# Twenty hold points a pair instead of twelve for GpSimd's gathers in a graph-network kernel

## The chip, the cores and the metric

One core of a Trainium2 chip. The metric is the device time of one execution in microseconds (us); a kernel's time is the median of its runs. Engines are named as in the profile: PE is TensorE (PEld its weight loads, which overlap its matmuls), DVE VectorE, ACT ScalarE, POOL GpSimd, SP SyncE.

## The reference

A layer of a graph network with 12,500 nodes and 400,000 edges, the edges sorted by their target node. For each edge the layer-normed features of both ends and the edge's own 32 numbers go through a small two-layer network; each node takes the maximum over its edges and adds it to its input.

```python
        e_feat = jnp.concatenate([x[rol], x[col], edge_attr], axis=-1)
        h = jax.nn.relu(e_feat @ W1 + b1)
        v = h @ W2 + b2
        x_cand = jax.ops.segment_max(v, col, num_segments=num_nodes)
        return jnp.maximum(x_cand, x[:, -v.shape[-1]:])
    edge_index = jnp.stack([src, dst])
    h = jnp.maximum(_layernorm(x, axis=-1), 0.0)
    x = x + _L0_gnn_ref(h, edge_index, edge_attr_32, L0_gnn_W1, L0_gnn_b1, L0_gnn_W2, L0_gnn_b2)
```

The first five lines are the body of `_L0_gnn_ref`, whose `x` is the normed `h`; `rol` and `col` are the two ends of an edge.

## The kernel before, in words

The sorted edges are cut into four stripes, and each stripe into 196 chunks of 512 edges; one step works on a chunk of all four stripes, that is on 16 columns of 128 edges. The loop takes two chunks at a time, a pair, so there are 98 pairs. Most time is spent on one job: getting `h[src]`, the rows of the edges' source nodes, which lie anywhere in memory.

That job is split between two ways. Twelve of a chunk's 16 columns are gathered by GpSimd with one indirect DMA for each column of 128 rows (`gather`, line 179). The other four are computed on TensorE (`tile`, line 344): one-hot rows `hot`, made by VectorE and ScalarE from keys, are multiplied with the whole table `hs`, in 14 matmuls a tile (seven groups of rows, each in two parts that add up to full precision); VectorE then masks and reduces the result (lines 351 and 352). In 34 of the chunks, always the second one of a pair, a fifth column is computed this way, so that GpSimd gathers 11. The prediction calls a pair with that extra tile a nine-tile pair, the others eight-tile pairs. An eight-tile pair has 24 gathers, a nine-tile pair 23.

Rows of both ways are turned by VectorE into `ht` (lines 368 and 371) and multiplied with the first weights.

TensorE's order in one pair is fixed by hand (`manual_schedule`); each engine runs its instructions in the order in which the code issues them. For a pair it is:

- three groups of first-layer matmuls, line 773: of the edges' own features (point `ea`), of the target windows, and of the rows (`ht`). Each is 8 matmuls in the program and 16 records in the profile, 48 records in all
- 8 transposes of the pair before, line 669 (`tr`)
- three tiles, the last three of the pair's first chunk, line 344 (`a1`, `a2`, `a3`)
- the second layer, line 807, 16 records, and 8 matmuls of the pair before, line 686 (`lv`)
- the four tiles of the second chunk (`b0` to `b3`), the extra tile of a nine-tile pair, and the first tile of the next pair (`n0`)

The names in brackets are points: `passes` notes the last matmul of a group under the pair's number and a name. GpSimd does nothing in the loop but issue gathers, two chunks ahead or more. It is kept to TensorE's pace by holds: `hold` looks up a gather's number in its pair (0 to 23, first chunk and then second) in the table `HELD`, which names a point and how many pairs back it lies; after the loop each held gather gets a semaphore wait for that point. The pair's first gathers are held by points three pairs back, the others by points two pairs back. So gathers run well ahead of their use: the latest of them are used about one pair later.

Each gather also waits for the gather eight before it (one of eight DMA semaphores, `DMASW0` to `DMASW7`) and, where it starts a new buffer of three columns (there are 14), for the VectorE instruction that read the buffer last.

Of the kernel before, what the change touches and what calls it, by code (L numbers as in the profile page):

```python
# [46 lines left out]
A1 = 7  # L47
# [16 lines left out]
LATE = NCH - 8  # L64
PIECE = 2 * A0
GP = 3
HELD = {0: (3, 'b1'), 2: (3, 'b2'), 4: (3, 'b3'), 6: (3, 'n0'), 8: (2, 'ea'), 10: (2, 'ht'), 12: (2, 'tr'), 14: (2, 'a1'), 16: (2, 'a2'), 18: (2, 'a3'), 20: (2, 'lv'), 22: (2, 'b0')}
BANKS = 7
SOON = {(3, 0): 'a0', (3, 6): 'a2', (4, 0): 'a3', (4, 6): 'b0', (5, 0): 'b1', (5, 6): 'b2'}
ROUND = 12582912.0  # L70
# [13 lines left out]
def gnn_kernel(ctx, tc, x, src, src_mm, src_x, src_t, dst, dst_ext, lo, lo_c, ends_b, edge_attr, weights, w1, w2, b2, out):  # L84
# [129 lines left out]
    def passes(iteration, name, ins):  # L214

        passed[iteration, name] = ins

    def hold(c, i, ins):

        at = HELD.get(i + c % 2 * (K - MM))  # L220
        if at and c // 2 - at[0] >= 0:
# [9 lines left out]
    def bank(name):  # L231

        return ring[0].tile([P, C], F32, name=name, tag="bank", bufs=BANKS)
# [94 lines left out]
    def tile(c, m):  # L328

        if c not in MMC or m == MM and c not in MMX:  # L330
            return
        if m == 0:
            mm_rows[c] = early.tile([P, MM, D], F32, name="gm", bufs=4)
        if m < MM:
            hot = [hots[c][:, k, m * P:(m + 1) * P] for k in range(A1)]
            mask, row = masks[c][:, m], mm_rows[c][:, m]
        else:
            _, mask, spaces = extras.pop(c)
            hot = [spaces[k // 2][:, k % 2 * P:(k % 2 + 1) * P] for k in range(A1)]
            row = gh[c][-1][:, SOME - 1]  # L340
        po = bank("pv")[:, :D * A0]
        for k in range(A1):
            for part in range(2):
                ins = nc.tensor.matmul(po, hot[k], hs[:, part, k].rearrange("p f a -> p (f a)"),  # L344
                                 start=(k == 0 and part == 0), stop=(k == A1 - 1 and part == 1))
        if m == 0 and c % 2 == 0:
            passes(c // 2 - 2, "n0", ins)
        passes(c // 2 - 1, "ab"[c % 2] + str(m), ins)
        of_group = po.rearrange("p (f a) -> p f a", a=A0)
        one = early.tile([P, D, A0], F32, name="one", bufs=2)  # L350
        nc.vector.tensor_tensor(one, of_group, mask[:, None, :].to_broadcast([P, D, A0]), op=ALU.mult)  # L351
        nc.vector.tensor_reduce(row, one, axis=AX.X, op=ALU.max)  # L352
# [210 lines left out]
    with tc.tile_pool(name="edges", bufs=3) as pool, tc.tile_pool(name="edges_ps", bufs=1, space=PSUM) as ps:  # L563
# [260 lines left out]
        load_wide(wide[0][1], (pen_d, 0), 0, LOAD * C, nc.sync)  # L824
        one_hots_act(3)
        tile(2, 0)
        one_hots(3, 0, 2)
        tile(2, 1)
        one_hots(3, 2, BY_ACT.start)
        mask_of(3)  # L830
        raw_turn(3)
        tile(2, 2)
        make_block(0)
        tile(2, 3)
# [19 lines left out]
        for c in range(0, NCH - 4, 2):  # L854
# [14 lines left out]
            if c == LATE + 2:  # L869
                ea = pool.tile([P, LOAD * C], F32, name="ea", bufs=2)  # L870
# [123 lines left out]
        c = NCH - 4  # L994
# [192 lines left out]
```

## Time and profile before

| | us |
|---|---|
| median of 3 runs | 3587.91 |
| lowest and highest run | 3581.08, 3589.38 |
| the profiled execution, own time | 3575.96 |
| its span, first to last instruction | 3574.1 |
| PE, busy | 3241.7 |
| DVE, busy | 2223.2 |
| POOL, busy | 2207.4 |
| ACT, busy | 1578.5 |

The mean granted clock of TensorE over the span is 0.944 of full speed. Busy times of PE come from matmuls whose ends are modelled, so a busy PE isn't a PE at its peak. In the rows of the timeline the first number is the start in us from the span's beginning, the second the length in us, and the bracket says how long the engine was idle before the row's first instruction and what ended that; `x16` counts records. In a row of the windows view the stretch is followed by its length, each engine's busy time with its count of instructions, the granted clock, the DMA engines' share and GB/s.

### The profile page before, as it was taken

How to read it: one execution, taken by the hardware profiler on the slowest of the kernel's cores; microseconds unless marked ns; L12 is line 12 of the kernel's file. 1: busy time of each engine (PE TensorE's matmuls, PEld its weight loads, DVE VectorE, ACT ScalarE, POOL GpSimd, SP SyncE). 2: the span in 40 equal slices, each digit the busy share in tenths (PEclk: the TensorE clock that was granted, in tenths of full speed). 3: DMA queues.
4: the chain of work that ended last, by engine and by line, in shares of the span. 5: the costliest groups of instructions: out<-in, count | busy, mean ns of one | idle time of the engine just before them, and what ended most of it. 6: DMA issues, size and time to landing. Idle time of an engine off the chain costs nothing.

```text
span 3574.1 us, 55458 instructions
## 1 busy us (share of the span) xinstructions
PE 3241.7 (91%) x19141; PEld 2547.7 (71%) x19141; DVE 2223.2 (62%) x4215; ACT 1578.5 (44%) x2470; POOL 2207.4 (62%) x2337
## 2 busy tenths in 40 slices
PE   5899999989999998999999999989999999999987
PEld 3577777777777776777777767777777777777765
DVE  5456666666666666666666666656665666666655
ACT  3344444443534444444443434444444444444443
POOL 6666666665666666666666666666666666666662
PEclk8899999999999999999999999999999999999997
DMA  5322222222222222222222222222222222222222
GB/s 175 99 60 62 53 64 62 62 50 62 64 62 53 61 63 65 50 66 60 62 50 70 57 56 58 59 59 61 60 62 59 60 61 61 63 65 49 59 58 65
DMA packets 178819, 227.49 MB, mean 64 GB/s; under 512 B 109621, under 2 KB 150373, under 8 KB 165734
## 3 DMA queue, kind: packets, MB, share of 16 engines
q10 hardware_dynamic: 29828, 108.01, 9.6%
q0 software_dynamic: 74336, 38.21, 8.5%
q1 hardware_dynamic: 74370, 77.70, 7.0%
q8 instruction: 151, 2.47, 0.3%
q14 instruction: 134, 1.10, 0.1%
HBM read 212.23 MB, written 11.46 MB: 63 GB/s over the span
## 4 chain that ended last, share of the span: by engine, by line
PE 81%; issue 10%; DVE 6%; another core or an unknown queue 2%; SPq 1%; DMA 1%; ACT 1%; DVEq 0%; ACTq 0%
PE pv L344 60%; PE ph L773 10%; PE pv L686 4%; PE pv L669 3%; PE pv L807 3%; DVE hot L304 1%; DVE one L351 1%; DVE last L650 1%; DVE sm L815 1%; DMA top_d<-wo 0%; DVE ht L368 0%; SPq L616 0%; SPq L707 0%; SPq L625 0%
## 5 line engine op out<-in xcount | busy, mean ns | idle before, releaser
L179 POOL DMA_INDIRECT gh<-h_d,src_i x2291 | 2169.8, 947 | 1296.3 <-issue 560.0
L344 PE MATMUL pv<-hs,hot 128*128 128x448 f32 x10752 | 2373.0, 378 | 97.5 <-issue 83.9
L344 PEld LDWEIGHTS pv<-hs,hot 128*128 128x128 f32 x10752 | 2089.1, 196 | 345.7 <-issue 159.7
L351 DVE TENSOR_TENSOR one<-pv,mask 128x448 f32<-128x448 f32 x768 | 472.3, 615 | 1219.7 <-remote 464.7
L798 ACT ACTIVATE hid<-ph,wt 128x512 f32<-128x512 f32 x392 | 250.0, 688 | 1124.6 <-remote 498.2
L352 DVE TENSOR_REDUCE gm<-one 128x32 f32<-128x448 f32 x768 | 476.2, 620 | 26.5
L304 DVE TENSOR_TENSOR hot<-kb,consts 128x1024 fp32r<-128x1024 f16 (+1 forms) x379 | 447.5, 1199 | 0.0
L318 ACT ACTIVATE hot<-away,ones 128x512 fp32r<-128x512 f32 x582 | 421.6, 724 | 45.0 <-remote 26.1
L317 ACT ACTIVATE away<-kb,key_n 128x512 f32<-128x512 f16 x582 | 416.0, 715 | 0.0
L692 ACT ACTIVATE wo<-pv 128x256 f32<-128x256 f32 x95 | 36.6, 385 | 631.2 <-remote 439.2
L815 DVE TENSOR_TENSOR_SCAN sm<-pb,sm,pv 128x512 f32<-128x512 bf16 x195 | 243.6, 1249 | 16.5 <-remote 9.0
L686 PEld LDWEIGHTS pv<-so,last 128*128 128x128 f32 x768 | 107.5, 191 | 159.5 <-issue 148.5
L773 PE MATMUL ph<-ht,wt 32*64 32x512 f32 x1568 | 197.3, 618 | 21.0 <-issue 13.0
L686 PE MATMUL pv<-so,last 128*128 128x256 f32 x768 | 148.6, 304 | 74.3 <-issue 67.7
L368 DVE STREAM_TRANSPOSE ht<-gh 128x96 f32<-128x96 f32 x774 | 207.4, 269 | 1.2
L661 ACT ACTIVATE sb<-sm,wt 128x512 f32<-128x512 f32 x196 | 138.1, 715 | 138.7 <-issue 87.6
L669 PEld LDWEIGHTS pv<-ident,sb 128*128 128x128 f32 x782 | 91.8, 150 | 120.3 <-issue 95.1
L773 PE MATMUL ph<-of,qf 32*64 32x512 f32 x1552 | 147.6, 600 | 19.6 <-issue 17.5
L669 PE MATMUL pv<-ident,sb 128*128 128x128 f32 x782 | 126.4, 298 | 30.4 <-issue 24.4
L773 PEld LDWEIGHTS ph<-ht,wt 32*64 32x64 f32 x1568 | 62.7, 135 | 114.1 <-issue 98.5
L642 ACT ACTIVATE of<-of,ones 128x512 f32<-128x512 f32 x194 | 140.6, 725 | 6.3
L641 ACT ACTIVATE of<-db,below 128x512 f32<-128x512 int32 x194 | 137.4, 708 | 0.0
(115 smaller groups left out, 1328.2 us busy)
## 6 DMA issues: line engine op xcount, KB each, us to landing
ea<-in_edge_attr SPq DMA_DIRECT2D x49, 1024.0 KB
db<-in_dst_ext ACTq DMA_DIRECT2D x48, 1024.0 KB
gh<-h_d,src_i POOLq DMA_INDIRECT x2291
pb<-pen_d ACTq DMA_DIRECT2D x48, 512.0 KB
kb<-key_d ACTq DMA_DIRECT2D x47, 512.0 KB
top_d<-wo SPq DMA_DIRECT2D x752, 3.0 KB
qf<-q_d SPq DMA_DIRECT2D x392, 16.0 KB
q_d<-qs SPq DMA_DIRECT2D x6, 512.0 KB
```

The costliest lines, as they stand in the source:

```text
L179: ins = nc.gpsimd.indirect_dma_start(out=parts[-1][:, i, :], out_offset=None, in_=h_d[:, :], in_offset=bass.IndirectOffsetOnAxis(ap=src_i[ ...
L304: nc.vector.tensor_tensor(hot_of(c)[:, start:stop], keys[c][:, None, :].to_broadcast([P, n, MM * P]), key_ps[:, start:stop, None].to_broad ...
L317: nc.scalar.activation(away, keys[c], AF.Square, bias=key_n[:, k:k + 1])
L318: nc.scalar.activation(hot_of(c)[:, k], away, AF.Relu, bias=ones, scale=-1.0)
L344: ins = nc.tensor.matmul(po, hot[k], hs[:, part, k].rearrange("p f a -> p (f a)"), start=(k == 0 and part == 0), stop=(k == A1 - 1 and par ...
L351: nc.vector.tensor_tensor(one, of_group, mask[:, None, :].to_broadcast([P, D, A0]), op=ALU.mult)
L352: nc.vector.tensor_reduce(row, one, axis=AX.X, op=ALU.max)
L669: passes(c // 2 + 1, "tr", nc.tensor.transpose(px[:, j, :], sb[:, j * P:(j + 1) * P], ident))
L686: ins = nc.tensor.matmul(pw[:, x % n], last[x][:, j].rearrange("p s w -> p (s w)"), sos[x][0][:, j], start=(j == 0 and x < n), stop=(j == ...
L773: ins = nc.tensor.matmul(ph[s][x * HID:(x + 1) * HID], w[g], e[g], start=start, stop=stop)
L798: nc.scalar.activation(hid[k], of, AF.Relu, bias=b1c)
L815: nc.vector.tensor_tensor_scan(found[:, :n], loaded.pop(c)[2][:, :n], pv[:, :n], -LOW if before is None else before[:, C - 1:C], op0=ALU.a ...
```

## The change

The table has twenty entries in place of twelve. A name with a minus sign is a new kind of point: the middle of a tile, noted after the fourth of the tile's seven groups, that is after its eighth matmul of 14. `tile` notes both kinds. Gathers 7, 11, 18 and 23 of a pair stay without a hold. (The extra tile has no points of its own in the table.)

```diff
-HELD = {0: (3, 'b1'), 2: (3, 'b2'), 4: (3, 'b3'), 6: (3, 'n0'), 8: (2, 'ea'), 10: (2, 'ht'), 12: (2, 'tr'), 14: (2, 'a1'), 16: (2, 'a2'), 18: (2, 'a3'), 20: (2, 'lv'), 22: (2, 'b0')}
+HELD = {0: (3, 'b1'), 1: (3, 'b2-'), 2: (3, 'b2'), 3: (3, 'b3-'), 4: (3, 'b3'), 5: (3, 'n0-'), 6: (3, 'n0'),
+        8: (2, 'ea'), 9: (2, 'ht'), 10: (2, 'tr'), 12: (2, 'a1-'), 13: (2, 'a1'), 14: (2, 'a2-'), 15: (2, 'a2'),
+        16: (2, 'a3-'), 17: (2, 'a3'), 19: (2, 'lv'), 20: (2, 'b0-'), 21: (2, 'b0'), 22: (2, 'b1-')}
...
             for part in range(2):
                 ins = nc.tensor.matmul(po, hot[k], hs[:, part, k].rearrange("p f a -> p (f a)"),
                                  start=(k == 0 and part == 0), stop=(k == A1 - 1 and part == 1))
-        if m == 0 and c % 2 == 0:
-            passes(c // 2 - 2, "n0", ins)
-        passes(c // 2 - 1, "ab"[c % 2] + str(m), ins)
+            if k in (A1 // 2, A1 - 1):
+                at = "" if k == A1 - 1 else "-"
+                if m == 0 and c % 2 == 0:
+                    passes(c // 2 - 2, "n0" + at, ins)
+                passes(c // 2 - 1, "ab"[c % 2] + str(m) + at, ins)
```

TensorE's, VectorE's, ScalarE's and SyncE's orders stay as they are, apart from line numbers; so does the order of the gathers. What changes is which gathers carry a wait for PE. Two stretches of GpSimd's queue show it, for chunks 80 and 81 (one pair). First gathers 3 to 10, which run around the end of a pair and the first-layer matmuls of line 773. In the rows `gh_14212` and so on are the buffers that the gather fills, `h_d` is the table and `src_i` the indices; in the brackets stand the semaphores, of which `PE_49` is the hold. Before:

```order
L179 DMA gh_14212<-h_d_63,src_i_70 128x32 [waits DMASW5_49,DVE_49]
L179 DMA gh_14212<-h_d_63,src_i_70 128x32 [waits DMASW6_49,PE_49]
L179 DMA gh_14212<-h_d_63,src_i_70 128x32 [waits DMASW7_49]
L179 DMA gh_14216<-h_d_63,src_i_70 128x32 [waits DMASW0_49,DVE_49,PE_49]
L179 DMA gh_14216<-h_d_63,src_i_70 128x32 [waits DMASW1_49]
L179 DMA gh_14216<-h_d_63,src_i_70 128x32 [waits DMASW2_49,PE_49]
L179 DMA gh_14220<-h_d_63,src_i_70 128x32 [waits DMASW3_49,DVE_49]
L179 DMA gh_14220<-h_d_63,src_i_70 128x32 [waits DMASW4_49,PE_49]
```

The same eight gathers in the changed kernel:

```order
L181 DMA gh_14212<-h_d_63,src_i_70 128x32 [waits DMASW5_49,DVE_49,PE_49]
L181 DMA gh_14212<-h_d_63,src_i_70 128x32 [waits DMASW6_49,PE_49]
L181 DMA gh_14212<-h_d_63,src_i_70 128x32 [waits DMASW7_49,PE_49]
L181 DMA gh_14216<-h_d_63,src_i_70 128x32 [waits DMASW0_49,DVE_49,PE_49]
L181 DMA gh_14216<-h_d_63,src_i_70 128x32 [waits DMASW1_49]
L181 DMA gh_14216<-h_d_63,src_i_70 128x32 [waits DMASW2_49,PE_49]
L181 DMA gh_14220<-h_d_63,src_i_70 128x32 [waits DMASW3_49,DVE_49,PE_49]
L181 DMA gh_14220<-h_d_63,src_i_70 128x32 [waits DMASW4_49,PE_49]
```

Gathers 3, 5 and 9 (first, third and seventh row) have a new hold: gather 3 by the middle of `b3`, gather 5 by the middle of `n0`, the tile just ahead of the first-layer matmuls, and gather 9 by `ht`, the end of those matmuls, which held gather 10 before.

Then gathers 14 to 21, which run from the tiles `a1` to `a3` to the second chunk's first tile. Before:

```order
L179 DMA gh_14224<-h_d_63,src_i_70 128x32 [waits DMASW0_49,PE_49]
L179 DMA gh_14228<-h_d_63,src_i_70 128x32 [waits DMASW1_49,DVE_49]
L179 DMA gh_14228<-h_d_63,src_i_70 128x32 [waits DMASW2_49,PE_49]
L179 DMA gh_14228<-h_d_63,src_i_70 128x32 [waits DMASW3_49]
L179 DMA gh_14232<-h_d_63,src_i_70 128x32 [waits DMASW4_49,DVE_49,PE_49]
L179 DMA gh_14232<-h_d_63,src_i_70 128x32 [waits DMASW5_49]
L179 DMA gh_14232<-h_d_63,src_i_70 128x32 [waits DMASW6_49,PE_49]
L179 DMA gh_14236<-h_d_63,src_i_70 128x32 [waits DMASW7_49,DVE_49]
```

The same eight in the changed kernel:

```order
L181 DMA gh_14224<-h_d_63,src_i_70 128x32 [waits DMASW0_49,PE_49]
L181 DMA gh_14228<-h_d_63,src_i_70 128x32 [waits DMASW1_49,DVE_49,PE_49]
L181 DMA gh_14228<-h_d_63,src_i_70 128x32 [waits DMASW2_49,PE_49]
L181 DMA gh_14228<-h_d_63,src_i_70 128x32 [waits DMASW3_49,PE_49]
L181 DMA gh_14232<-h_d_63,src_i_70 128x32 [waits DMASW4_49,DVE_49]
L181 DMA gh_14232<-h_d_63,src_i_70 128x32 [waits DMASW5_49,PE_49]
L181 DMA gh_14232<-h_d_63,src_i_70 128x32 [waits DMASW6_49,PE_49]
L181 DMA gh_14236<-h_d_63,src_i_70 128x32 [waits DMASW7_49,DVE_49,PE_49]
```

Gather 18 (fifth row) loses its hold to gather 17, which now waits for `a3`; gather 19 takes over `lv` from gather 20. At each point from `ht` to `lv` GpSimd stands one gather further back than before; it makes up for that between `b0` and `b1`, where gathers 20 to 23 go in place of 22 and 23.

## The prediction

> **What bounds the kernel now.** I began with the page: busy times, granted clock, the chain that ended last.
>
> ```profile
> span 3574.1 us, 55458 instructions
> PE 3241.7 (91%) x19141; PEld 2547.7 (71%) x19141; DVE 2223.2 (62%) x4215; ACT 1578.5 (44%) x2470; POOL 2207.4 (62%) x2337
> PE 81%; issue 10%; DVE 6%; another core or an unknown queue 2%; SPq 1%; DMA 1%; ACT 1%; DVEq 0%; ACTq 0%
> PE pv L344 60%; PE ph L773 10%; PE pv L686 4%; PE pv L669 3%; PE pv L807 3%; DVE hot L304 1%; DVE one L351 1%; DVE last L650 1%; DVE sm L815 1%; DMA top_d<-wo 0%; DVE ht L368 0%; SPq L616 0%; SPq L707 0%; SPq L625 0%
> ```
>
> PE sets the end: 81% of the chain is its own work, and 10%, some 357 us of 3574.1, is "issue", time in which PE waits for nothing that the profile names. GpSimd isn't on the chain, so the change can matter in one way only: if the moment at which a gather runs lengthens or shortens PE's "issue" time. To see whether it does, I put PE's timeline beside GpSimd's where a pair begins, in two places. The first follows a nine-tile pair:
>
> ```profile
> 881.76 2.96 PE L344 MATMUL pv<-hs,hot 128*128 128x448 f32 x14
> 884.65 1.11 PE L773 MATMUL ph<-ea,wt 32*64 32x512 f32 x16
> 887.41 1.10 PE L669 MATMUL pv<-ident,sb 128*128 128x128 f32 x8
> 879.40 0.95 POOL L179 DMA_INDIRECT gh<-h_d,src_i  x1 [0.30 <-issue]
> 884.99 0.94 POOL L179 DMA_INDIRECT gh<-h_d,src_i  x1 [4.64 <-PE pv L344]
> 886.24 0.95 POOL L179 DMA_INDIRECT gh<-h_d,src_i  x1 [0.30 <-issue]
> ```
>
> The 48 records of line 773 go from 884.65 to 887.41, in 2.76 us. GpSimd had been idle for 4.64 us ahead of them, held by `n0`. The second place follows an eight-tile pair:
>
> ```profile
> 1168.18 1.11 PE L773 MATMUL ph<-ea,wt 32*64 32x512 f32 x16
> 1169.09 2.75 PE L773 MATMUL ph<-of,qf 32*64 32x512 f32 x12
> 1173.06 1.09 PE L669 MATMUL pv<-ident,sb 128*128 128x128 f32 x8
> 1166.14 0.94 POOL L179 DMA_INDIRECT gh<-h_d,src_i  x1 [0.30 <-DVE mask L323]
> 1167.39 0.95 POOL L179 DMA_INDIRECT gh<-h_d,src_i  x1 [0.30 <-issue]
> 1168.64 0.94 POOL L179 DMA_INDIRECT gh<-h_d,src_i  x1 [0.31 <-issue]
> 1171.46 0.94 POOL L179 DMA_INDIRECT gh<-h_d,src_i  x1 [1.87 <-remote]
> ```
>
> Here gathers start 2.0 and 0.8 us ahead of the block, and the same 48 records take 4.88 us. Gathers follow each other every 1.25 us where nothing holds them (0.95 us and a gap of 0.30). Windows of both beginnings, of a third, and of whole pairs, price this:
>
> ```profile
> 884.60:888.20 3.60, 3.60 (x56) 1.86 (x56) 3.41 (x5) 0.00 (x0) 2.60 (x3) 1.00 0.32 79
> 1168.20:1174.00 5.80, 5.61 (x58) 2.35 (x58) 3.51 (x8) 0.00 (x0) 3.01 (x5) 1.00 0.31 81
> 1310.50:1316.20 5.70, 4.93 (x58) 2.29 (x57) 5.06 (x10) 1.01 (x2) 3.23 (x4) 1.00 0.30 78
> 845.10:884.60 39.50, 35.02 (x207) 27.63 (x206) 23.85 (x46) 15.81 (x25) 22.89 (x25) 0.96 0.25 54
> 884.60:917.30 32.70, 31.19 (x193) 24.77 (x192) 19.74 (x35) 15.82 (x25) 20.80 (x22) 0.95 0.28 70
> 1135.50:1168.20 32.70, 29.76 (x196) 23.97 (x196) 20.47 (x37) 16.04 (x25) 21.61 (x23) 1.00 0.23 55
> 1168.20:1203.70 35.50, 32.34 (x193) 25.73 (x192) 21.24 (x40) 16.15 (x25) 21.89 (x24) 0.95 0.25 67
> 1310.50:1343.90 33.40, 30.84 (x193) 24.08 (x192) 21.04 (x40) 16.16 (x25) 20.81 (x22) 1.00 0.26 66
> ```
>
> A nine-tile pair (PE x207) takes 39.50 us, the one behind it 32.70, an eight-tile pair behind another 35.50. So a nine-tile pair and its follower take 72.2 us, two eight-tile pairs 71.0: the extra tile costs 1.2 us, though its 14 matmuls last 2.96 us. Its work is nearly paid back by the clean beginning behind it. PE has time to lose and to win in these blocks.
>
> **The change, part by part.** *Waits on GpSimd.* Five gathers of a pair (1, 5, 13, 17 and 19) go from one wait to two, and the second is an instruction of its own on GpSimd's queue.
>
> ```profile
> L179 POOLq EVENT_SEMAPHORE  x1525: 17/17/43, 61.2 to 3516.6; - x191
> ```
>
> At 17 ns each that is 5 x 17 = 85 ns a pair, 8 us over 95 pairs, inside the 0.30 us gaps: nothing. Behind a waiting gather only later gathers queue. They are used about a pair, some 36 us, later; 24 of them need 24 x 1.25 = 30 us. So lateness of a few us reaches nobody, and I take 0; if that cover were gone, PE would wait in front of line 773 for as long as the gathers are late.
>
> *Signals on PE.* Eight mid-tile matmuls of a pair now signal, about 760 in all.
>
> ```profile
> 1830.19 11.38 PE L344 MATMUL pv<-hs,hot 128*128 128x448 f32 x56
> 1844.21 2.96 PE L344 MATMUL pv<-hs,hot 128*128 128x448 f32 x14
> L344 PE MATMUL pv<-hs,hot 128*128 128x448 f32 x10752 | 2373.0, 378 | 97.5 <-issue 83.9 <-DVE hot L304 7.8 <-ACT qs L505 1.1
> ```
>
> A matmul lasts 0.378 us, so inside one tile the 13 steps take (2.96 - 0.378) / 13 = 0.199 us. Over four tiles, with three ends that signal already, the 55 steps take (11.38 - 0.378) / 55 = 0.200 us. The 0.001 us by which they differ makes 0.06 us for three signals, 0.02 each: at most 760 x 0.02 = 15 us, at least nothing. I take 0, since the second figure is the first within its rounding.
>
> *Gather 5 moves up to the block of line 773.* Today it follows gather 4 and may start 1.55 us behind the end of `b3`; in a nine-tile pair two whole tiles then pass without a gather, and the block behind them is clean. Now it waits for the middle of `n0`. The hold at the end of `n0` released its gather 0.34 us behind the block's first record (884.99 against 884.65). Six matmuls earlier that is 6 x 0.2 = 1.2 us less, so gather 5 will start about 0.9 us ahead of the block, in every pair. Behind the 34 nine-tile pairs this is new. Its price there: nothing in the block at 1847.10, which had gathers close ahead and was clean.
>
> ```profile
> 1844.66 0.95 POOL L179 DMA_INDIRECT gh<-h_d,src_i  x1 [0.30 <-issue]
> 1845.91 0.95 POOL L179 DMA_INDIRECT gh<-h_d,src_i  x1 [0.30 <-issue]
> 1847.10 1.11 PE L773 MATMUL ph<-ea,wt 32*64 32x512 f32 x16
> 1848.01 1.06 PE L773 MATMUL ph<-of,qf 32*64 32x512 f32 x16
> ```
>
> At most it is 5.70 - 3.60 = 2.1 us, the beginning at 1310.50, whose pair also follows a nine-tile pair and had gathers close ahead. Between these I take what reached that pair's end: 33.40 - 32.70 = 0.7 us. 34 x 0.7 = 24 us (0 to 71). In the other 61 pairs a gather runs in those last two microseconds already: 0.
>
> *Gather 9 leaves the block.* Held by `ht`, it no longer follows gather 8, so one gather fewer runs beside lines 773 and 669. The beginnings above give (5.80 - 3.60) / (5 - 3) = 1.1 us for a gather in that stretch, the most that this can bring; the least is nothing, since the gather isn't saved but runs later, and the tiles' stretch ahead of the next block gets it. I take 0.2 us, nearer to nothing, as an estimate for the 61 pairs whose beginning isn't clean: -12 us (0 to -67).
>
> *The stretch `a1` to `lv`.* GpSimd stops at `a3` as before, one number lower (gather 17, not 18), with as many gathers behind `ht` (9 to 16, before 10 to 17). PE's blocks at lines 807 and 686 meet the same traffic: 0.
>
> Sum: 3575.96 + 24 - 12 = 3588 for a profiled execution. The median of the runs lies 12 us above the profiled one (3587.91 against 3575.96), so the forecast is **3600 us**, slower by 0.34%.
>
> **The rivals.** *Even spacing pays, faster.* If GpSimd's bursts of two gathers are what starves PE, single gathers with gaps shorten the blocks: half of the 1.1 us in 61 pairs is 34 us, 3554 us. For it speaks the price per gather in the windows; against it that GpSimd has its waits in few places already:
>
> ```profile
> POOL gh L179 <- issue: 560.0, 1760, 3.4
> POOL gh L179 <- remote: 289.8, 181, 3.5
> POOL gh L179 <- PE pv L344: 238.8, 147, 4.7
> ```
>
> 1760 of 2291 gathers start 0.3 us behind the one before: held or not, GpSimd mostly runs late and doesn't stop. New holds that are passed when it arrives change nothing. It decides from the point at which most of the new holds bind.
>
> *Nothing comes of it.* If a gather costs PE the same wherever it runs, only their number counts, and that stays: 3588 us. The nearly free extra tile, in a chunk with one gather fewer, speaks for it; the clean beginnings against it.
>
> *GpSimd becomes the bound, much slower.* A hold that binds costs 1.3 to 1.9 us of idling instead of 0.3. If eight more did so in each of 95 pairs, at 1.0 us, GpSimd's 36 us a pair would become 44 and its lead of one pair be used up: 3588 + 8 x 95 = 4348 us. Against it: a hold binds only while GpSimd is ahead of PE.
>
> *The clock.* The granted clock of the pairs above goes from 0.95 to 1.00. If shorter stalls kept it at 1.00 throughout, the mean of 0.944 leaves (1 - 0.944) x 3574.1 = 200 us: 3388 us.
>
> ```profile
> core 0: 3574.1 us, clock 0.944
> ```
>
> [...]
>
> **How the numbers follow.** The forecast has 0.38; even spacing 0.31; nothing 0.24; GpSimd the bound 0.04; the clock 0.03. About 0.3% (11 us) is what a measurement of this kernel can tell from no change. Slower is then 0.38 + 0.04 = 0.42, the same 0.24, faster 0.31 + 0.03 = 0.34. The likeliest case's own range is 3599 to 3659 (all of the 71 us and none of the gain). The range is 3545 to 3650: below it the far half of the even-spacing case and the clock, above it the dearest mid-`n0` gathers and GpSimd as the bound.
>
> **What would show it.** Right: in the changed trace a gather starts about 0.9 us ahead of nearly every block of line 773; behind nine-tile pairs the block takes over 2.76 us in many cases, and those pairs grow from 32.7 towards 33.4 us; elsewhere the gap behind gather 8 grows and the beginnings shrink by a few tenths. Wrong: if the blocks behind nine-tile pairs stay clean, the 24 us fall away; if beginnings behind eight-tile pairs get clean too, or the "issue" share falls well under 10%, even spacing was the point; if PE waits for `ht` from line 368, lateness of gathers reached it.

## The result, and the profile after

The changed kernel takes 3551.84 us (median of 4 runs, 3547.15 to 3553.86) against 3584.64 us (4 runs, 3581.08 to 3589.38) of the kernel before on the same chip: a ratio of 0.9916 with a 95% interval of 0.9902 to 0.9930, that is 30 us faster (25 to 35) by the ratio, which this document goes by; the medians are 33 us apart. The prediction said 3600 us, slower by 0.34%. The time lies inside its range, but the sign is wrong: the range reaches so far down only for the rival of even spacing.

The page of the changed kernel, with its span, the busy times and the clock:

```profile
span 3552.1 us, 55930 instructions
PE 3301.4 (93%) x19141; PEld 2554.6 (72%) x19141; DVE 2230.3 (63%) x4215; ACT 1566.6 (44%) x2470; POOL 2208.2 (62%) x2337
core 0: 3552.1 us, clock 0.942
```

The clock is what it was (0.944 before), and every engine has the same instructions to run. PE's busy time is 60 us longer for the same 19,141 matmuls, as stretched matmuls have longer records: the `ht` matmuls of the first layer last 679 ns in the mean and are busy for 316.8 us (line 777), 618 ns and 197.3 us before (line 773). What moved are PE's stalls. The next two fences show the wait lists of PE's weight loads: the line that waited, what for ("issue": for nothing that the profile names), us in total, times, and the longest. Before:

```profile
PEld ph L773 <- issue: 242.1, 548, 15.7
PEld pv L344 <- issue: 200.6, 288, 3.3
PEld pv L686 <- issue: 148.5, 207, 1.7
PEld pv L669 <- issue: 95.1, 121, 1.6
```

And after (four lines lower in the code: 777, 346, 690, 673):

```profile
PEld ph L777 <- issue: 319.3, 635, 8.2
PEld pv L346 <- issue: 141.7, 181, 3.2
PEld pv L673 <- issue: 93.0, 111, 2.0
PEld pv L690 <- issue: 87.6, 115, 1.8
```

The first-layer matmuls lost 77 us (242.1 to 319.3). The tiles won 59 (200.6 to 141.7), and the matmuls of line 690 won 61 (148.5 to 87.6). The prediction put both of these at nothing. (Weight loads overlap matmuls, 2554.6 and 3301.4 us busy in a span of 3552.1, so these sums don't add up to the time won: the two profiles are 22 us apart.)

GpSimd's own list, whose rows for before stand in the prediction (1760 gathers behind "issue", 147 held by a tile):

```profile
POOL gh L181 <- issue: 520.4, 1599, 3.4
POOL gh L181 <- PE pv L346: 348.0, 319, 2.7
POOL gh L181 <- remote: 142.2, 85, 4.8
```

The tiles' points now stop a gather 319 times instead of 147. Still, 1599 of 2291 gathers start straight behind the one before.

PE's timeline where a pair begins shows how a block looks when it is stretched. GpSimd's gathers stand in the fence below it:

```profile
1334.44 1.09 PE L777 MATMUL ph<-ea,wt 32*64 32x512 f32 x9
...
1337.37 2.56 PE L777 MATMUL ph<-ht,wt 32*64 32x512 f32 x9
1340.29 1.01 PE L777 MATMUL ph<-ht,wt 32*64 32x512 f32 x2 [0.36 <-issue]
1341.73 2.57 PE L777 MATMUL ph<-ht,wt 32*64 32x512 f32 x4 [0.43 <-issue]
1344.23 1.97 PE L673 MATMUL pv<-ident,sb 128*128 128x128 f32 x8
...
1355.48 1.09 PE L811 MATMUL pv<-hid,wt 64*32 64x512 f32 x16
1356.50 1.22 PE L690 MATMUL pv<-so,last 128*128 128x256 f32 x8
1357.55 2.17 PE L346 MATMUL pv<-hs,hot 128*128 128x448 f32 x10
```

```profile
1331.96 0.95 POOL L181 DMA_INDIRECT gh<-h_d,src_i  x1 [0.30 <-issue]
1333.21 0.95 POOL L181 DMA_INDIRECT gh<-h_d,src_i  x1 [0.30 <-issue]
1336.01 0.94 POOL L181 DMA_INDIRECT gh<-h_d,src_i  x1 [1.85 <-PE pv L346]
...
1353.99 0.95 POOL L181 DMA_INDIRECT gh<-h_d,src_i  x1 [1.22 <-PE pv L346]
1355.24 0.95 POOL L181 DMA_INDIRECT gh<-h_d,src_i  x1 [0.30 <-issue]
1356.50 0.95 POOL L181 DMA_INDIRECT gh<-h_d,src_i  x1 [0.30 <-issue]
```

The block of line 777 takes 9.8 us (1334.44 to 1344.23) instead of 2.76, with gathers 2.5 and 1.2 us ahead of it. The block of line 690 in the same pair takes 1.05 us, its unstretched time, and has gathers 2.5, 1.3 and 0.0 us ahead. So here gathers close ahead of a block do not by themselves lengthen it, and the prediction's price for a gather rests on the view that they do. This is one pair; counts over all pairs follow below.

### The profile page after: what moved, and what is told of

Read it like the earlier page. It is cut to its first block, busy times and chain, and to the rows that moved or that the text cites. A ratio compares the mean times of both kernels' runs of the same rounds, so it can differ in the third digit from the quotient of the medians.

```text
span 3552.1 us, 55930 instructions
## 1 busy us (share of the span) xinstructions
PE 3301.4 (93%) x19141; PEld 2554.6 (72%) x19141; DVE 2230.3 (63%) x4215; ACT 1566.6 (44%) x2470; POOL 2208.2 (62%) x2337
## 5 line engine op out<-in xcount | busy, mean ns | idle before, releaser
L346 PE MATMUL pv<-hs,hot 128*128 128x448 f32 x10752 | 2319.5, 374 | 84.7 <-issue 76.9
L346 PEld LDWEIGHTS pv<-hs,hot 128*128 128x128 f32 x10752 | 2062.9, 194 | 293.5 <-issue 123.7
L802 ACT ACTIVATE hid<-ph,wt 128x512 f32<-128x512 f32 x392 | 241.3, 688 | 1174.2 <-remote 439.0
L777 PE MATMUL ph<-ht,wt 32*64 32x512 f32 x1568 | 316.8, 679 | 44.6 <-issue 30.3
L777 PEld LDWEIGHTS ph<-ht,wt 32*64 32x64 f32 x1568 | 83.3, 139 | 206.9 <-issue 178.1
L673 PEld LDWEIGHTS pv<-ident,sb 128*128 128x128 f32 x782 | 109.9, 171 | 137.9 <-issue 93.0
L777 PE MATMUL ph<-of,qf 32*64 32x512 f32 x1552 | 172.8, 602 | 19.5 <-issue 16.8
L673 PE MATMUL pv<-ident,sb 128*128 128x128 f32 x782 | 150.4, 338 | 26.6 <-issue 20.5
L690 PEld LDWEIGHTS pv<-so,last 128*128 128x128 f32 x768 | 99.8, 189 | 95.6 <-issue 87.6
L690 PE MATMUL pv<-so,last 128*128 128x256 f32 x768 | 126.2, 298 | 14.5 <-issue 12.9
```

Of the source, the lines that this page charges most:

```text
L673: passes(c // 2 + 1, "tr", nc.tensor.transpose(px[:, j, :], sb[:, j * P:(j + 1) * P], ident))
L690: ins = nc.tensor.matmul(pw[:, x % n], last[x][:, j].rearrange("p s w -> p (s w)"), sos[x][0][:, j], start=(j == 0 and x < n), stop=(j == ...
L777: ins = nc.tensor.matmul(ph[s][x * HID:(x + 1) * HID], w[g], e[g], start=start, stop=stop)
L802: nc.scalar.activation(hid[k], of, AF.Relu, bias=b1c)
```

## The experiments

There were 18 runs, in five jobs; some tables ran in several. A fact that only the first job brought out governs how all are read: **the kernel before does not always have the stretches.** In three jobs it took 3003 to 3004 us, with no such stretch in any trace of the job, and in two it took 3570 to 3577 us, with stretches in the traces as in the first measurement. The first kind is called quiet here. Three theories were set against each other. A: the late gathers are held one gather earlier against PE's order (at `tr`, whose hold goes from gather 12 to gather 10, it is two, more than the section on the change says). B: it is the single gathers and the points in the middle of a tile. C: the prediction's own sum.

All tables are put into the changed kernel's code, and their computation is unchanged.

**Four tables, first job (quiet; before 3004.28 us, 33 runs).** The shift alone, and the middle points alone:

```diff
-HELD = {0: (3, 'b1'), 1: (3, 'b2-'), 2: (3, 'b2'), 3: (3, 'b3-'), 4: (3, 'b3'), 5: (3, 'n0-'), 6: (3, 'n0'),
-        8: (2, 'ea'), 9: (2, 'ht'), 10: (2, 'tr'), 12: (2, 'a1-'), 13: (2, 'a1'), 14: (2, 'a2-'), 15: (2, 'a2'),
-        16: (2, 'a3-'), 17: (2, 'a3'), 19: (2, 'lv'), 20: (2, 'b0-'), 21: (2, 'b0'), 22: (2, 'b1-')}
+HELD = {0: (3, 'b1'), 2: (3, 'b2'), 4: (3, 'b3'), 6: (3, 'n0'), 8: (2, 'ea'), 9: (2, 'ht'), 10: (2, 'tr'), 13: (2, 'a1'), 15: (2, 'a2'), 17: (2, 'a3'), 19: (2, 'lv'), 21: (2, 'b0')}
```

> Twelve holds, all at ends of groups, none in the middle of a tile, but tied to the gathers of the changed table: gather 9 waits for ht, 10 for tr, 13, 15 and 17 for a1, a2 and a3, 19 for lv, 21 for b0. So between ht and b0 GpSimd stands one gather further back than before. Theory A (what counts is that one gather fewer is out when PE reaches lines 773, 807 and 686; the mid-tile points are beside the point): about the changed kernel's time, ratio 0.990 to 0.995. Theory B (what counts is that gathers come singly, which needs the mid-tile points): no gain, 0.998 to 1.003. Theory C (my own sum: the gather let go in the middle of n0 costs 24 us, the shift gains 12 us): 0.995 to 0.998, faster than the changed kernel would be without its early half's cost.

```diff
-        8: (2, 'ea'), 9: (2, 'ht'), 10: (2, 'tr'), 12: (2, 'a1-'), 13: (2, 'a1'), 14: (2, 'a2-'), 15: (2, 'a2'),
-        16: (2, 'a3-'), 17: (2, 'a3'), 19: (2, 'lv'), 20: (2, 'b0-'), 21: (2, 'b0'), 22: (2, 'b1-')}
+        8: (2, 'ea'), 10: (2, 'ht'), 12: (2, 'tr'), 13: (2, 'a1-'), 14: (2, 'a1'), 15: (2, 'a2-'), 16: (2, 'a2'), 17: (2, 'a3-'), 18: (2, 'a3'), 20: (2, 'lv'), 21: (2, 'b0-'), 22: (2, 'b0'), 23: (2, 'b1-')}
```

> Twenty holds with the mid-tile points, but each end of a group keeps the gather that it held before (ht 10, tr 12, a1 14, a2 16, a3 18, lv 20, b0 22); the mid-tile points hold the odd gathers between. Theory A (the shift counts): no gain, 0.998 to 1.003. Theory B (single gathers count): about the changed kernel's ratio, 0.990 to 0.995. Theory C: the price of the mid-n0 gather without the shift's gain, 1.004 to 1.010.

The change's late half (gathers 8 to 22) with the early half of before, and the reverse:

```diff
-HELD = {0: (3, 'b1'), 1: (3, 'b2-'), 2: (3, 'b2'), 3: (3, 'b3-'), 4: (3, 'b3'), 5: (3, 'n0-'), 6: (3, 'n0'),
+HELD = {0: (3, 'b1'), 2: (3, 'b2'), 4: (3, 'b3'), 6: (3, 'n0'),
```

> The changed table from gather 8 on (ea to the middle of b1), the table of before for gathers 0 to 7 (ends of b1, b2, b3 and n0). Theory A: nearly the whole gain, 0.990 to 0.995, and line 686's block of 8 records short as in the changed kernel (mean about 1.4 us against 2.4 before). Theory B: about half of the gain, 0.994 to 0.998. Theory C: more than the changed kernel gains, by the 24 us that the mid-n0 gather costs, about 0.985.

```diff
-        8: (2, 'ea'), 9: (2, 'ht'), 10: (2, 'tr'), 12: (2, 'a1-'), 13: (2, 'a1'), 14: (2, 'a2-'), 15: (2, 'a2'),
-        16: (2, 'a3-'), 17: (2, 'a3'), 19: (2, 'lv'), 20: (2, 'b0-'), 21: (2, 'b0'), 22: (2, 'b1-')}
+        8: (2, 'ea'), 10: (2, 'ht'), 12: (2, 'tr'), 14: (2, 'a1'), 16: (2, 'a2'), 18: (2, 'a3'), 20: (2, 'lv'), 22: (2, 'b0')}
```

> The changed table for gathers 0 to 7 (with the middles of b2, b3 and n0), the table of before from gather 8 on. Theory A: no gain, 0.998 to 1.003. Theory B: about half of the gain, 0.994 to 0.998. Theory C: slower by the mid-n0 gather's 24 us, 1.004 to 1.010, with longer blocks of line 773 behind nine-tile pairs.

Measured, in this order: 0.9996 (0.9987 to 1.0005), 1.0000 (0.9991 to 1.0010), 1.0001 (0.9992 to 1.0010), 1.0003 (0.9994 to 1.0012). This doesn't tell the theories apart, since what they are about is absent here.

**The changed kernel itself and no holds at all, second job (quiet; before 3004.03 us, 33 runs).** The changed kernel as it is:

> The changed kernel itself once more, against the kernel before on the same chip. If the 0.9916 of the first measurement belongs to the kernel, it comes again here whatever the chip: 0.990 to 0.993. If it belongs to the stretches in which TensorE issues a matmul only every 0.70 us (theory of the bursts), it comes again only where these stretches are in the trace, which a time of the kernel before near 3585 us tells; on a chip where the kernel before takes about 3004 us the ratio is 1.000 to within 0.001, as for the four tables before. The prediction's own sum would say 1.003 on either.

The first two tables again:

> The shifted late half alone, points at the ends of groups only (as in the first of the four tables). Where the kernel before takes near 3585 us: theory A (the late gathers are held one gather earlier against PE's order) 0.991 to 0.994; theory B (it is the single gathers and the middle points) 0.998 to 1.002; theory C (the prediction's sum) about 0.997, the gather that leaves the block of the out projection being the only term that is left. Where it takes about 3004 us: 1.000 by all.

> Single gathers at middle points, but no gather held earlier in the late half. Where the kernel before takes near 3585 us: theory A 0.998 to 1.002; theory B 0.991 to 0.994; theory C about 1.005, the early half's gather moved up being the only term. Where it takes about 3004 us: 1.000 by all.

```diff
-HELD = {0: (3, 'b1'), 1: (3, 'b2-'), 2: (3, 'b2'), 3: (3, 'b3-'), 4: (3, 'b3'), 5: (3, 'n0-'), 6: (3, 'n0'),
...
+HELD = {}
```

> No gather is held by PE at all (the six of the first pairs and the waits on buffers stay). Says what any table of holds is worth. Where the kernel before takes about 3004 us GpSimd issues gathers back to back already, so 0.998 to 1.002 if holds are worth nothing there; over 1.01 if gathers then run ahead and meet the other transfers. Where it takes near 3585 us: 1.02 or more if pacing is what the tables buy (theory of even spacing), about 1.00 if only the places of the bursts matter, under 0.99 if holding a gather costs more than it gives.

Measured: 1.0002 (0.9993 to 1.0011), twice 1.0001 (0.9992 to 1.0010), and without any hold 1.0005 (0.9996 to 1.0014). In a quiet job the table is worth nothing in any form. The changed kernel's page there, chain and wait list of PE, shows what is missing:

```profile
PE 94%; DMA 3%; POOL 1%; DVE 1%; issue 1%; ACT 0%; POOLq 0%; ACTq 0%; SPq 0%; DVEq 0%
PE hp L495 <- DVE h L453: 18.9, 1, 18.9
PE pv L346 <- ACT hid L802: 6.9, 1, 6.9
PEld ph L777 <- issue: 125.6, 478, 0.8
```

"issue" is 1% of the chain, PE's own list has no "issue" row, and the longest such wait of a weight load at line 777 is 0.8 us (8.2 above). The extra tile of a nine-tile pair, nearly free before, costs its full time here: 31.95 us against 29.11 (means over 34 and 60 pairs).

**Three tables again and one with every hold a pair later, third job (quiet; before 3002.78 us, 26 runs).**

> The shifted late half alone, on whichever chip comes. In the profile of the kernel before on the first chip, register moves on SP that wait for nothing take up to 0.70 us in 238 places and TensorE issues a pair of weight load and matmul every 0.70 us in its stretches; on the two chips since, no such move takes over 0.05 us and no stretch is there. So the expectation hangs on the time of the kernel before: near 3004 us, 1.000 by all; near 3585 us, theory A (late gathers one earlier against PE's order) 0.991 to 0.994, theory B (single gathers and middle points) 0.998 to 1.002, theory C (the prediction's sum) 0.997.

> Single gathers at middle points without the shift. Kernel before near 3004 us: 1.000 by all. Near 3585 us: theory A 0.998 to 1.002, theory B 0.991 to 0.994, theory C 1.005.

> The change's late half with the early half of before. Kernel before near 3004 us: 1.000 by all. Near 3585 us: 0.988 to 0.992 if the whole gain is the late half's (theory A, and the prediction's plus of 24 us for the early half would then be a cost the change pays); about 0.997 by theory C; 0.995 if each half brings part (theory B).

```diff
-HELD = {0: (3, 'b1'), 1: (3, 'b2-'), 2: (3, 'b2'), 3: (3, 'b3-'), 4: (3, 'b3'), 5: (3, 'n0-'), 6: (3, 'n0'),
-        8: (2, 'ea'), 9: (2, 'ht'), 10: (2, 'tr'), 12: (2, 'a1-'), 13: (2, 'a1'), 14: (2, 'a2-'), 15: (2, 'a2'),
-        16: (2, 'a3-'), 17: (2, 'a3'), 19: (2, 'lv'), 20: (2, 'b0-'), 21: (2, 'b0'), 22: (2, 'b1-')}
+HELD = {0: (2, 'b1'), 1: (2, 'b2-'), 2: (2, 'b2'), 3: (2, 'b3-'), 4: (2, 'b3'), 5: (2, 'n0-'), 6: (2, 'n0'),
+        8: (1, 'ea'), 9: (1, 'ht'), 10: (1, 'tr'), 12: (1, 'a1-'), 13: (1, 'a1'), 14: (1, 'a2-'), 15: (1, 'a2'),
+        16: (1, 'a3-'), 17: (1, 'a3'), 19: (1, 'lv'), 20: (1, 'b0-'), 21: (1, 'b0'), 22: (1, 'b1-')}
```

> The changed kernel's table with every hold one pair later, so that each gather may start only some 29 us (a pair of matmul groups on a chip without the slow stretches) later than now. Says how far the holds are from deciding the end. If the gathers' results are not needed for a whole pair after they land, 1.000 where the kernel before takes 3004 us; if the holds then reach the path, each pair gains a wait on PE and the ratio is 1.02 or more.

Measured: 1.0002 (0.9992 to 1.0011), 1.0004 (0.9994 to 1.0014), 1.0003 (0.9993 to 1.0013), and 1.0039 (1.0025 to 1.0053) with the holds a pair later. The last lies between the two values that were expected. With the tables as they were, lateness of gathers reaches nobody; with holds that let a gather start a whole pair of 30 us later it begins to. That costs 12 us in the whole kernel, and PE's waits for `ht` at the first layer, 4.3 us in the changed kernel's quiet trace, are one place where it shows:

```profile
PE ph L775 <- DVE ht L373: 13.7, 8, 4.5
```

**Copies beside the kernel, fourth job (with stretches; before 3569.51 us, 13 runs).** Each pair issues one or four copies of 2 MB from memory to memory, whose result is read by nobody:

```diff
+            for k in range(1):
+                junk = junks.tile([P, 4096], F32, name="junk")
+                nc.scalar.dma_start(junk, ea_v[:, (c + k) * C // 2:(c + k) * C // 2 + 4096])
```

> The kernel before with one copy of 2 MB from memory to memory a pair (98 pairs less three), issued by ACT, whose result nobody reads; the kernel's output is unchanged. Theory of supply (instructions come late when the DMA engines are busy): PE's gaps over 0.6 us, 26 on a chip without the stretches and 481 on the first, go over 100, SP register moves near 0.7 us appear, and the time goes over 1.01. Theory of the chip: no gap of that kind, 1.000 to 1.005.

> The changed kernel with the same copy of 2 MB a pair. Against the kernel before with the copy: theory of supply 0.99 to 0.995 if the changed places of the gathers keep the supply clear where TensorE's groups are short, as on the first chip; theory of the chip 1.000.

> The kernel before with four such copies a pair, 8 MB, which at the rate of 8,192-byte packets in the trace (309 ns each on one of 16 engines) is some 20 us of all 16 engines in a pair of 30 us: an estimate from these rows. Theory of supply: over 1.05, with stretches of 0.7 us a pair of matmuls. Theory of the chip: the time may grow because gathers land later, but no pair of matmuls takes 0.7 us and no SP register move does.

> The changed kernel with four copies a pair. Against the kernel before with four copies: theory of supply under 0.995; theory of the chip 0.998 to 1.002, or over 1.002 if gathers that land late make the holds reach the path, as they did when each hold was put a pair later (1.004).

With one copy: the kernel before 3570.94 us, 1.0002 (0.9982 to 1.0022), the changed one 3550.69 us, 0.9942 (0.9923 to 0.9961). The job came with stretches, so it cannot say whether traffic makes them where there are none. It shows no sign that traffic adds to them: from one matmul's start to the next PE takes over 0.6 us 493 times with the copy, 481 times in the profile of the first measurement and 26 to 40 times in quiet traces (the expectations and this document call such a step a gap), though the queue that the copies use goes from 9.6% to this share of the DMA engines and memory traffic from 63 GB/s to this:

```profile
q10 hardware_dynamic: 43652, 309.34, 25.5%
HBM read 413.56 MB, written 212.79 MB: 175 GB/s over the span
```

The changed kernel gains under this traffic too: its four runs (3546 to 3554 us) all lie below the ten of before with the copy (3557 to 3586).

With four copies: 4749.03 us and 4775.58 us, 1.329 and 1.338 of the kernel before. That growth is another matter, as rows of PE's and ACT's lists for the first of the two show:

```profile
PE pv L345 <- ACT hid L799: 1070.2, 93, 25.2
ACT hid L799 <- DMA top_d<-wo: 1530.9, 53, 36.8
ACT hid L799 <- DMA junk<-in_edge_attr: 902.3, 30, 36.1
```

ACT issues the copies, and between the issue of one and of the next it stands for over 3 us 217 times, 2501 us in all. Its first-layer activation (line 799) comes behind them in its queue, so PE waits for ACT. The ACT rows name the DMA to which the profile puts the end of a wait; the activation itself reads neither the stores nor the copies. Gaps near 0.70 us (0.69 to 0.73) become rarer in that trace, 49 in place of 186. The changed kernel is 0.6% slower than the kernel before under these waits. The last expectation allowed for that if late gathers reach the path, but whether they do is not shown.

**Each half alone, fifth job (with stretches; before 3577.02 us, 13 runs).** The tables of the first job's third and fourth run:

> The change's late half with the early half of before. Where the kernel before takes 3560 to 3590 us: the prediction's terms 0.997 (minus 12 us); if the whole gain is the late half's and the early half costs 24 us as predicted, 0.983 to 0.988; if both halves bring part of it, 0.993 to 0.997. Where it takes 3004 us: 1.000 as in two runs of this table before.

> The change's early half with the late half of before. Where the kernel before takes 3560 to 3590 us: the prediction's terms 1.007 (plus 24 us), with the block of line 775 longer behind nine-tile pairs; if the gain is the late half's alone, 1.000 or more; if the early half brings the gain, 0.990 to 0.995, and the block of line 688 and the first tile of the second chunk become shorter as in the changed kernel. Where it takes 3004 us: 1.000.

Late half 3541.71 us, 0.9908 (0.9891 to 0.9925): 33 us faster (27 to 39). Early half 3586.29 us, 1.0024 (1.0010 to 1.0037): 9 us slower (4 to 13). The whole gain is the late half's; the early half costs a little. The two together, -24 us, agree within their intervals with the -30 us (25 to 35) of the change, which was measured in another job. The wait lists of PE's weight loads, late half first:

```profile
PEld ph L775 <- issue: 349.6, 655, 8.6
PEld pv L344 <- issue: 119.8, 166, 2.2
PEld pv L671 <- issue: 90.3, 119, 1.7
PEld pv L688 <- issue: 81.6, 102, 5.0
```

Early half:

```profile
PEld pv L344 <- issue: 265.4, 361, 3.9
PEld ph L775 <- issue: 222.2, 550, 8.9
PEld pv L688 <- issue: 122.2, 148, 2.9
PEld pv L671 <- issue: 102.5, 133, 1.7
```

Against the kernel before (first layer 242.1, tiles 200.6, line 686 148.5), the late half has the pattern of the changed kernel, only stronger: plus 108, minus 81, minus 67. The early half has its cost in the tiles, plus 65 (in `a1` to `a3`, by the table below).

The same from PE's records, as mean us from one block's first matmul to the next block's, over 94 pairs of one profile each ("before" is the profile that the prediction reads, so the columns come from different jobs):

| block (lines before the change) | before | early half | late half | changed | changed, quiet |
|---|---|---|---|---|---|
| first layer, 773 | 4.11 | 4.09 | 5.91 | 5.85 | 2.76 |
| - behind a nine-tile pair | 2.88 | 2.99 | 4.33 | 3.48 | 2.76 |
| - behind an eight-tile pair | 4.81 | 4.71 | 6.80 | 7.19 | 2.76 |
| transposes, 669 | 1.34 | 1.62 | 1.57 | 1.52 | 0.85 |
| tiles `a1` to `a3` | 9.35 | 9.95 | 9.45 | 9.62 | 8.83 |
| second layer, 807 | 1.12 | 1.21 | 1.08 | 1.10 | 1.07 |
| 686 | 2.39 | 1.97 | 1.29 | 1.38 | 1.06 |
| tiles `b0` to `n0` | 17.52 | 17.10 | 16.16 | 16.11 | 15.56 |
| sum | 35.83 | 35.95 | 35.46 | 35.57 | 30.14 |

In the late half 2.50 us a pair are won (at 686, in the tiles behind it and at 807), and 2.13 are lost at 773, at 669 and in the tiles `a1` to `a3`, 85% as much. 0.37 x 94 = 35 us remain. That is the gain.

Whether the shift (A) or the middle points (B) does this within the late half was to be tried by the first two tables, but all three jobs in which they ran were quiet, so it stays open. The late half alone measures below the changed kernel (0.9908 against 0.9916), but the intervals overlap: it is not shown to be better.

## Why the prediction was wrong, step by step

*PE's "issue" time is what the change can touch: right, and more than was said.* Where that time is absent, the change is worth nothing (1.0002). But the prediction took the 357 us for the kernel's own; three quiet jobs show that they aren't.

*Waits on GpSimd and signals on PE: right.* The quiet runs bound both together: the upper end of 1.0011 allows 3 us in 3004, and the prediction allowed up to 15 for the signals alone. That GpSimd's lateness reaches nobody was right too, and the lead is known now: with holds a pair later 12 us are lost.

*Gather 5 moves up, +24 us: the gather moved as foretold, its price was wrong.* The early half costs 9 us, and not where the step put it, so that the right sign is luck in part. It named the block of line 773 behind nine-tile pairs, 0.7 us each; the early half alone moves that block from 2.88 to 2.99 us, 34 x 0.11 = 4 us, and 24 of 34 blocks stay under 2.9 us (30 before). Yet in that trace a gather does start 0.85 to 0.89 us ahead of 27 of these 34 blocks, where 26 had none in the last 2.5 us before: the step said 0.9. The changed kernel does show the 0.6 us that the step foretold (2.88 to 3.48), which at first sight confirms it. But the late half alone gives 4.33: the blocks lost their cleanness to another part of the change. The early half holds gathers 1 and 3 anew as well; what each of the three does was not tried.

*Gather 9 leaves the block, -12 us: failed.* With the late half, of which this is a part, the block behind eight-tile pairs did not shrink by 0.2 us but grew by 2.0 (4.81 to 6.80).

*The stretch `a1` to `lv`, 0: this is the step that turned the sign.* It argued that as many gathers run behind `ht` as before, so that lines 807 and 686 meet the same traffic. The blocks of line 686 went from 2.39 to 1.29 us, and those left unstretched (under 1.1 us) from 28 of 94 to 64; the first tile behind them went from 4.14 to 3.13 us. The count of gathers in a stretch, on which the step rested, does not tell this. For the tiles `b0` to `n0`, where the late half wins 1.36 us a pair, the sum had no term at all.

Under all three terms lies one premise: that a gather close to a block has a price, which can be read from three chosen windows (1.1 us a gather). The division itself is circular: the second window is 2.20 us longer, and at one gather every 1.25 us that alone lets nearly two more run in it, whatever made it longer. Over all pairs the premise looked sound in the trace before: of the 94 blocks of line 773, the 27 with no gather in the 2.5 us ahead took 2.79 us in the mean, those with two 4.85. But 26 of the 27 stand behind nine-tile pairs. In the changed kernel the seven with no gather ahead took 8.0 us and the 51 with two 5.6; in the early half alone 33 of the 34 blocks behind nine-tile pairs have a gather ahead, and they stay nearly clean. So the missing gathers alone do not explain the clean blocks before; what does is not known. The other reading from chosen windows, that the extra tile costs 1.2 us, does not hold over all pairs either: a nine-tile pair and its follower take 38.57 + 32.80 = 71.4 us in the mean, two eight-tile pairs behind eight-tile pairs 2 x 36.20 = 72.4.

*Even spacing pays, 3554 us: nearest in time, but not by its mechanism.* It expected shorter blocks at the beginning of the pair, and these became longer; the gain comes from the second half of the pair. That the time falls so near 3554 us, and within the range, is luck. It also asked that most of the new holds bind; PE's points, over all lines, stop 487 gathers instead of 240, which is 247 of some 760 new holds. Whether single gathers as such matter is open (B above).

*No clock term in the sum: right* for this change, 0.942 against 0.944, but no run shows what lowers the clock. In the prediction's windows it is 1.00 in the block at 1310.50, which is 2.1 us longer than the clean one, and 0.95 or 0.96 in three of the five whole pairs; where all stretches are gone, in the quiet jobs, it is 0.992 over the span, and with four copies a pair, where PE is busy for 70% of the span, 0.843. So the rival's link between stalls and clock is not refuted. *GpSimd as the bound: did not come*; the quiet profile has it at 1% of the chain.

What remains argued and not shown is why gathers held elsewhere move the stretches. A reading that fits in part, a guess that no run shows: something limits how many instructions get through in a time, and PE stalls where it issues most. In the prediction's first window PE issues 56 matmuls and as many weight loads in 3.60 us, 31 a us, where the whole core's mean is 55,458 / 3574 = 15.5. A stall at one such place then leaves less to stall for at the next, as losses of 85% of what was won suggest, and also this: in the changed kernel the 50 pairs whose first-layer block takes over 5 us have 1.19 us at line 690, the other 44 have 1.60. But a cause behind both would look the same. And the tiles, at 28 matmuls and weight loads in 2.96 us, issue less than 10 a us and have stretches too (200.6 us in the list of before).

## What to carry to other kernels

Before a stall that the profile gives no reason for is priced or moved, the same kernel should be run in several jobs: if its time differs by more than any edit brings (3004 against 3577 us here), the stall belongs to the condition and an edit's worth with it. A price read from a few windows where two things always occur together (no gather, and a nine-tile pair ahead) is no price until it has been counted over all windows and seen under a change. And when stalls shrink at one place, the other places should be counted too: here they lost 85% of what was won.

## What the runs showed of the hardware that was not expected

*The same program takes 3003 to 3004 or 3570 to 3585 us.* Its granted clock is 0.990 to 0.993 in the first case; in the second it is 0.944 in the first profile and 0.945 to 0.954 in the later jobs. The record gives the number 14 to the chip of a quiet job and to that of a job with stretches, so the condition need not belong to one chip (whether the number names one piece of hardware is not told). Within a job it held: all 33 runs of the kernel before of the first job lie between 3000 and 3009 us.

*Not only PE is slow then, but not every engine.* SP's queue has register moves that wait for nothing. Its list at the line that stores the results, durations in ns as least/median/most, for the kernel before in the first measurement and for the changed kernel in a quiet job:

```profile
L707 SPq FUSED_REGOPS  x752: 2/37/762, 137.7 to 3505.2; - x188
L707 SPq MOVE top_d<-wo x752: 2/29/1532, 137.8 to 3505.3; - x188
```

```profile
L711 SPq FUSED_REGOPS  x752: 37/37/42, 105.5 to 2934.0; - x188
L711 SPq MOVE top_d<-wo x752: 29/29/29, 105.7 to 2934.1; - x188
```

A move that takes exactly 29 ns in a quiet run takes up to 1532 in the other. 238 register operations of SP last over 0.3 us there (135 us in all, a third of them within 0.69 to 0.71 us), and none in a quiet run. PE's gaps have the same step: of its 481 over 0.6 us, 186 lie between 0.69 and 0.73. VectorE, ScalarE and GpSimd show nothing of it: of their 3,091 semaphore waits as the trace records them three last over 0.3 us, as do three in the quiet one, and a gather takes 947 ns in the median, 944 in the quiet one. The step is close to the 721 ns that a TENSOR_LOAD of SP, which fills registers from the tile `lo_i`, takes in the median of the same trace:

```profile
L609 SPq TENSOR_LOAD <-lo_i x98: 5/721/995, 62.3 to 3509.5; - x98
```

So two of the engines now and then need about as long for an instruction as for one of these loads (0.69 to 0.73 us against 0.72); whether one waits for a read then is not shown. Most of SP's 238 long operations don't fall together with PE's: 68 overlap one of PE's gaps over 0.6 us, and some 44 would if they were shifted at random.

Late supply of instructions could look like this. But the transfers that the profile calls "instruction" don't show it. The page before has

```profile
q8 instruction: 151, 2.47, 0.3%
```

These are 151 transfers of 16,384 bytes, one for about every 254 records of PE and PEld. They take 1.1 us in the median, and 1.0 us in the quiet trace. Of PE's gaps over 0.6 us from the first of them to the last, 24 of 476 overlap one, fewer than the 45 that would at random. So PE's stretches aren't waits for these transfers; another lateness of supply isn't excluded. Whether the recording has a part in them is open as well: every run lists a span and a clock, so records were kept in all. Other DMA traffic (63 to 175 GB/s) left the time as it was (1.0002). SP's long operations were 279 with the copy and 238 without, a little above the 214 to 270 of the traces with stretches and no copies.
